# Planning a one-core decoder layer: the latest time of a load from HBM, taken from its readers or also from its queue

## The chip, the cores and the metric

The kernel runs on one core of a Trainium2 chip. The core has five engines that run side by side: TensorE (PE in the profile, with its weight loads as PEld), VectorE (DVE), ScalarE (ACT), GpSimd (POOL) and SyncE (SP). Each takes its instructions strictly in the order in which the program gives them; an instruction whose operand isn't ready holds up all that stand behind it on its engine. Two of them, SP and POOL, also issue the transfers (DMAs), which sixteen DMA engines carry out. The metric is the device time of one execution in microseconds (us).

## The reference

One decoder layer over x of shape (16, 256, 256), in float32: batch 16, length 256, width 256. Three parts follow each other, each with a residual and a layer norm after it:

- An attention by running sums: `z = x @ in_proj_w`, a causal convolution of four taps, then per head weights `p` (an exponential times a decay by position), cosines and sines of `x_val * theta`, running sums over the length of numerator and denominator, a normalisation, two small products, a gate, and `@ out_proj_w`.
- A cross attention by correlation: query, key and value are projected, correlated by Fourier transform, the five best shifts per head are chosen, and the value, shifted and weighted, goes through `Wo`.
- A mixture of eight experts of rank 64, run twice (forward and inverse): `xV * cumsum(yW)`, weighted by a router of two layers with softmax, then `U`, biases, and `@ W_O`. All its weights can be multiplied together beforehand.

## The kernel before, in words

The batch is taken in eight pairs (`NP`). For each pair the program text calls seven stages in turn: `front` (L602: xT load, input product in_ps, scores sc_ps, convolution zc, product g, broadcasts ph and gate), `body` (L668: broadcasts sn and ge, sines, scans, the products y and ss, and out_ps), `context` (L895: key and value spectra from ct, put away to HBM), `back` (L923: fetches them), `attention` (L1055), `router` (L1075) and `experts` (L1151: c_ps, v_ps, u_ps and the output). Ahead of them `fold_weights` (L815) loads twelve weight matrices as tiles `raw` and multiplies them into w_v, w_h, w_c, u_o and b_o (PE's w_ps); some twenty constants are loaded too.

None of these calls issues anything. Each engine is wrapped in `Later` (L68), and each call is noted as an `Op` with its engine, its rough duration (`cost`, L148), what it must follow and the tiles it uses. DMAs whose sources are all inputs of the program, that is loads from HBM such as xT, ct, x, raw and the constants, carry the mark `fetch` (set in `note`, L187). When all is noted, `work.run(PASSES)` plans and then issues everything in the planned order. A plan takes three passes:

- `forward` (L273) goes through time. For every engine it takes, of the operations whose inputs and tile buffers are there, the one with the smallest rank; one that is ready now goes before one that isn't. A load may not start more than 40 us (`AHEAD`, L122) before its latest time.
- `backward` (L424) goes through the plan from its end and gives each operation its latest time: what it can be moved to without making a reader late, and without making the next operation on its own engine late. SP's and POOL's queues count as engines here.
- The latest times are the ranks of the next pass. The first pass has only the ranks of `PLACES` (L39): for each stage, a length and a begin for each of the eight pairs, in units of a pair. The plan with the smallest planned end is issued.

What the order around the change depends on: the tile xT has one buffer, so the xT of a pair can be issued when the four in_ps products of the pair before are done. POOL issues the loads of constants, raw and x, and between them computes g, bothc, pp and t. SP issues xT, ct and all the broadcasts (ph, sn, ge, gate, vh, wb). The order of each queue is the plan's.

Of the kernel before, what the change touches and what calls it, by code (L numbers as in the profile page):

```python
# [36 lines left out]


PLACES = {  # L39
    "front": (1.0, 1.75, 3.7, 4.05, 4.2, 5.15, 5.65, 6.15, 8.0),  # L40
    "body": (0.5, -1.2, 1.45, 3.3, 1.4, 4.5, 4.55, 6.85, 7.75),
    "ctx": (0.9, 2.18, 0.8, 1.3, 1.6, 1.9, 1.3, 1.55, 2.55),
    "back": (0.5, -2.85, -2.95, -4.9, -5.5, -1.75, -3.0, -1.2, 2.1),
    "att": (0.1, -1.95, -2.75, -2.4, -4.5, -0.05, 0.45, 1.4, 4.15),
    "router": (1.45, 0.9, -3.2, 2.15, 2.1, 2.9, 4.65, 5.9, 4.9),
    "expert": (1.18, 4.05, 3.55, 5.65, 5.85, 7.4, 6.9, 9.8, 12.25),
    "fold": (2.75, 2.21),
}
EARLY, SLABS, XT_BUFS, ZC_BUFS, KBUFS, VBUFS, X_BUFS = 3, 17, 1, 4, 2, 3, 9
AHEAD = range(1, NP)  # L50
# [63 lines left out]
class Work:  # L114
# [309 lines left out]
    def backward(self, starts, span):  # L424

        free = dict.fromkeys(self.LEAD, span)
        late = {}
        for o in sorted(self.ops, key=lambda o: (-starts[o][1], -o.k)):
            end = min([span] + [late.get(q, span) - self.gap(o, q, q.pre[o]) for q in o.then])
            t = min(end - o.lat, free[o.eng] - o.dur + self.LEAD[o.eng])  # L430
            late[o], free[o.eng] = t, t
        return late

    def run(self, passes):
# [915 lines left out]
```

## Time and profile before

| what | value |
|---|---|
| median of 5 runs | 865.26 us (863.32 to 866.23) |
| the profiled execution | 865.74 us |
| its span in the profile | 864.0 us |
| mean granted TensorE clock | 0.979 |
| PE busy | 810.9 us, 94% of the span |
| DVE busy | 696.4 us, 81% |
| ACT busy | 596.0 us, 69% (129.6 of it loads of function tables) |
| POOL busy | 254.8 us, 29% |
| moved by DMA | 103.30 MB, mean 120 GB/s |

The profile comes from one execution. Almost all work carries the line of `give` (L452), where the planned operations are issued, so groups are told apart by tile: "in_ps<-xT,in_proj_w" is the product that writes in_ps and reads xT and in_proj_w. "A <-B x" in a list of waits says that A stood idle until x on B was done: microseconds in total, how often, and the longest. POOLq and SPq are the queues on which those engines issue DMAs. The time from a DMA's issue to its landing is part of the chain of waits where the chain runs through it.

### The profile page before, as it was taken

Reading aid. Unit: us, or ns where it says so; the run is one execution under the profiler, and the core shown is the slowest. Engines: PE = TensorE matmul, PEld = TensorE weight load, DVE = VectorE, ACT = ScalarE, POOL = GpSimd, SP = SyncE. Lnnn points to the kernel's source line nnn. Section 1 sums busy time; section 2 is a strip of 40 time slices with the busy share of each in tenths; the row PEclk is TensorE's granted clock in tenths of the full one; section 3 lists DMA queues with packets and bytes.
Section 4 is the critical chain, followed back from the end, with each engine's and each line's share of the span. In section 5 each row is a group of like instructions: output and inputs, shape, how many; then the busy total and the mean of one; then the engine's idle time right before and its main releaser. Section 6 shows DMA issues by size and latency. Waiting matters only on the chain.

```text
span 864.0 us, 12052 instructions
## 1 busy us (share of the span) xinstructions
PE 810.9 (94%) x4180; PEld 462.0 (53%) x4180; DVE 696.4 (81%) x1200; ACT 596.0 (69%) x874; POOL 254.8 (29%) x301
## 2 busy tenths in 40 slices
PE   4679999999989999999898999999999999999994
PEld 2236564464536654674353746665457357548453
DVE  6479799879899998999999799988979994472431
ACT  2859968699887999599658956769388933712601
POOL 8501455551503131424330212434122111221000
PEclk9879999999999999999999999999999999999998
DMA  7952787364745337435373536336351711130040
GB/s 233 344 121 57 184 246 202 124 186 118 191 103 129 92 86 171 111 85 147 98 171 90 131 74 142 115 77 157 84 127 45 173 46 49 38 86 1 24 98 25
DMA packets 57421, 103.30 MB, mean 120 GB/s; under 512 B 7616, under 2 KB 24032, under 8 KB 57360
## 3 DMA queue, kind: packets, MB, share of 16 engines
q1 hardware_dynamic: 47760, 71.85, 35.3%
q0 software_dynamic: 9600, 30.69, 11.0%
q8 instruction: 33, 0.54, 0.2%
q14 instruction: 28, 0.23, 0.1%
HBM read 28.06 MB, written 11.53 MB: 46 GB/s over the span
## 4 chain that ended last, share of the span: by engine, by line
PE 65%; ACT 13%; DVE 8%; issue 6%; DMA 5%; POOL 2%; POOLq 0%; SPq 0%; DVEq 0%; ACTq 0%
PE u_ps L452 11%; PE v_ps L452 10%; PE c_ps L452 9%; PE h_ps L452 6%; PE in_ps L452 4%; PE w_ps L452 3%; PE kv_ps L452 3%; PE wo_ps L452 3%; ACT L450 3%; ACT cs L452 3%; PE y L452 2%; PE ss L452 2%; PE out_ps L452 2%; DVE cs L452 2%; PE q_ps L452 2%
## 5 line engine op out<-in xcount | busy, mean ns | idle before, releaser
L450 ACT ACT_TABLE_LOAD x101 | 129.6, 1283 | 1.8
L452 PE MATMUL v_ps<-fxT,w_v 128*128 128x512 f32 x256 | 121.1, 602 | 2.8 <-DVE e L452 1.5
L452 PE MATMUL c_ps<-fcT,w_c 128*128 128x512 f32 x256 | 120.0, 601 | 0.1
L452 PE MATMUL u_ps<-u_o,e 128*128 128x256 f32 x512 | 116.4, 382 | 0.0
L452 PEld LDWEIGHTS u_ps<-u_o,e 128*128 128x128 f32 x512 | 95.6, 190 | 19.1 <-issue 6.7
L452 DVE TENSOR_TENSOR_SCAN cs<-again,cs 128x1024 f32<-128x1024 bf16 x32 | 77.3, 2416 | 0.0
L452 PEld LDWEIGHTS v_ps<-fxT,w_v 128*128 128x128 f32 x256 | 46.1, 190 | 54.6 <-issue 43.2
L452 DVE TENSOR_TENSOR_SCAN sn<-again,sn 128x1024 f32<-128x1024 bf16 x32 | 74.6, 2331 | 0.1
L452 PEld LDWEIGHTS c_ps<-fcT,w_c 128*128 128x128 f32 x256 | 46.5, 190 | 50.2 <-issue 46.8
L452 DVE SCALAR_TENSOR_TENSOR zc<-in_ps,pv,zc 128x510 f32<-128x510 f32 (+2 forms) x96 | 69.3, 734 | 2.2 <-ACT zc L452 1.7
L452 PE MATMUL h_ps<-fxT,w_h 128*128 128x512 f32 x128 | 61.5, 619 | 4.0 <-ACT fxT L452 4.0
L452 PE MATMUL kv_ps<-Wkv,specc 128*128 128x512 f32 x128 | 61.5, 614 | 3.2 <-ACT specc L452 3.2
L452 POOL TENSOR_TENSOR pp<-qf,kf 128x256 f32<-128x256 f32 (+1 forms) x32 | 43.7, 1385 | 69.5 <-ACT qf L452 64.8
L452 PE MATMUL in_ps<-xT,in_proj_w 128*128 128x512 f32 x128 | 62.9, 621 | 1.3 <-DVE sc L452 1.3
L452 DVE TENSOR_TENSOR e<-e,v_ps 128x512 f32<-128x512 f32 x64 | 43.0, 674 | 14.5 <-PE v_ps L452 14.5
L452 POOL DMA_DIRECT2D out<-x x16 | 11.7, 730 | 135.5 <-ACT x L452 123.0
L452 POOL TENSOR_TENSOR t<-vf,wf 128x256 f32<-128x256 f32 x32 | 22.7, 729 | 93.9 <-ACT wf L452 50.1
L452 ACT ACTIVATE ge<-sn 128x1024 f32<-128x1024 f32 x32 | 33.7, 1053 | 21.1 <-DVE cs L452 9.5
L452 ACT ACTIVATE sn<-sn,theta_col 128x512 f32<-128x512 f32 x64 | 44.5, 714 | 4.9 <-DMA sn<-zc 4.7
L452 DVE SCALAR_TENSOR_TENSOR cs<-cs,sn 128x1024 f32<-128x1024 f32 x32 | 42.1, 1316 | 6.9 <-ACT cs L452 6.8
L452 DVE TENSOR_TENSOR sn<-sn,ge 128x1024 f32<-128x1024 f32 x32 | 41.4, 1295 | 7.4 <-ACT sn L452 3.6
L452 ACT ACTIVATE zc<-in_ps,pv 128x512 f32<-128x512 f32 x32 | 24.5, 778 | 31.1 <-PE in_ps L452 31.1
(220 smaller groups left out, 1600.8 us busy)
## 6 DMA issues: line engine op xcount, KB each, us to landing
sn<-zc SPq DMA_DIRECT2D x64, 256.0 KB
ge<-g SPq DMA_DIRECT2D x64, 256.0 KB
wb<-fwT SPq DMA_DIRECT2D x64, 256.0 KB
ct<-in_ctx SPq DMA_DIRECT2D x16, 256.0 KB
xT<-in_xT SPq DMA_DIRECT2D x8, 512.0 KB
x<-in_x POOLq DMA_DIRECT2D x16, 256.0 KB, 3.8
ph<-sc SPq DMA_DIRECT2D x64, 64.0 KB
gate<-zc SPq DMA_DIRECT2D x64, 64.0 KB
```

The costliest lines, as they stand in the source:

```text
L450: self.scalar.preload_act_table_set(self.TABLES[table])
L452: call(*args, **kw)
```

## The change

In `backward`, an operation marked `fetch` gets its latest time from its readers alone. The latest time of the operation that stands behind it in its queue no longer bounds it, and it no longer bounds the operation that stands ahead of it. All other operations, copies out of SBUF and the fetches of spectra from HBM scratch in `back` among them, keep both bounds. Thirty-odd numbers of `PLACES`, the ranks of the first pass, are changed with it, by 0.05 to 0.25 units.

```diff
 PLACES = {
-    "front": (1.0, 1.75, 3.7, 4.05, 4.2, 5.15, 5.65, 6.15, 8.0),
-    "body": (0.5, -1.2, 1.45, 3.3, 1.4, 4.5, 4.55, 6.85, 7.75),
-    "ctx": (0.9, 2.18, 0.8, 1.3, 1.6, 1.9, 1.3, 1.55, 2.55),
-    "back": (0.5, -2.85, -2.95, -4.9, -5.5, -1.75, -3.0, -1.2, 2.1),
-    "att": (0.1, -1.95, -2.75, -2.4, -4.5, -0.05, 0.45, 1.4, 4.15),
-    "router": (1.45, 0.9, -3.2, 2.15, 2.1, 2.9, 4.65, 5.9, 4.9),
-    "expert": (1.18, 4.05, 3.55, 5.65, 5.85, 7.4, 6.9, 9.8, 12.25),
-    "fold": (2.75, 2.21),
+    "front": (1.0, 1.75, 3.7, 4.05, 4.2, 5.2, 5.65, 6.15, 8.1),
+    "body": (0.5, -1.2, 1.45, 3.3, 1.5, 4.5, 4.55, 6.85, 7.85),
+    "ctx": (0.9, 2.18, 0.8, 1.3, 1.6, 1.9, 1.3, 1.55, 2.65),
+    "back": (0.5, -2.85, -2.95, -4.9, -5.4, -1.75, -3.0, -1.2, 2.2),
+    "att": (0, -1.8, -3.0, -2.45, -4.75, -0.3, 0.2, 1.45, 4.2),
+    "router": (1.45, 0.9, -3.1, 2.15, 2.1, 2.9, 4.65, 5.9, 5.0),
+    "expert": (1.18, 3.85, 3.35, 5.45, 5.65, 7.2, 6.7, 9.6, 12.15),
+    "fold": (2.65, 2.26),
 }
...
         for o in sorted(self.ops, key=lambda o: (-starts[o][1], -o.k)):
             end = min([span] + [late.get(q, span) - self.gap(o, q, q.pre[o]) for q in o.then])
-            t = min(end - o.lat, free[o.eng] - o.dur + self.LEAD[o.eng])
-            late[o], free[o.eng] = t, t
+
+            t = end - o.lat if o.fetch else min(end - o.lat, free[o.eng] - o.dur + self.LEAD[o.eng])
+            late[o] = t
+            if not o.fetch:
+                free[o.eng] = t
         return late
```

## The prediction

> **What bounds the kernel now.** I read the page's busy times first, then TensorE's waits, then stretches of the span, then the chain and the timelines of the opening 60 us. Busy times, and the waits of TensorE (PE) and of the DVE between 20 and 60 us:
>
> ```profile
> span 864.0 us, 12052 instructions
> PE 810.9 (94%) x4180; PEld 462.0 (53%) x4180; DVE 696.4 (81%) x1200; ACT 596.0 (69%) x874; POOL 254.8 (29%) x301
> ...
> PE sc_ps L452 <- DMA xT<-in_xT: 11.6, 1, 11.6
> PE sc_ps L452 <- DMA w_sc<-in_w_sc: 8.5, 1, 8.5
> PE h_ps L452 <- ACT fxT L452: 4.0, 2, 3.1
> PE kv_ps L452 <- ACT specc L452: 3.2, 3, 2.0
> PE dft_ps L452 <- DMA f_dft<-in_f_dft: 2.6, 1, 2.6
> ...
> DVE g L452 <- DMA ph<-sc: 7.6, 1, 7.6
> ```
>
> PE is idle for 864.0 - 810.9 = 53.1 us, and its waits for DMA are all in the opening. Stretches (busy time of PE, PEld, DVE, ACT, POOL, then granted clock, DMA share, GB/s):
>
> ```profile
> 0.00:50.00 50.00, 24.42 (x96) 11.25 (x96) 26.85 (x68) 23.87 (x34) 30.94 (x52) 0.86 0.83 268
> 50.00:100.00 50.00, 50.00 (x281) 28.94 (x274) 43.44 (x44) 44.07 (x68) 9.79 (x12) 0.97 0.45 108
> ...
> 450.00:500.00 50.00, 45.91 (x259) 28.01 (x258) 44.20 (x57) 42.47 (x57) 6.76 (x7) 0.97 0.49 116
> ...
> 800.00:864.00 64.00, 52.69 (x178) 28.73 (x178) 20.86 (x50) 17.31 (x26) 3.53 (x5) 0.93 0.19 50
> ```
>
> The first 50 us hold 25.6 us of the idle time, the last 64 hold 11.3, the 750 between hold 16.2. So the kernel is bound by PE, and what can still be won lies mostly in the opening. There the chain of waits and the timelines read:
>
> ```profile
> 23.89 8.60 DMA raw<-in_V_fwd
> ...
> 36.46 12.16 DMA xT<-in_xT
> 48.66 1.93 PE sc_ps L452 x16
> ...
> 27.21 6.76 SPq L452 DMA_DIRECT2D ge<-g  x4
> 34.02 2.34 SPq L452 DMA_DIRECT2D ph<-sc  x3
> 19.47 0.73 POOL L452 DMA_DIRECT2D raw<-in_W_Q  x1
> ```
>
> PE's order is fixed, so it stood for 11.6 us until the second xT (pair 1's input) had landed. Its buffer was free when PE had finished pair 0's in_ps, at 26.5; its issue stood in SP's queue behind four ge, which wait for the DVE's g, and three ph: 10 us lost to the queue. Then it took 12.16 us among other traffic. After that idle time PE's granted clock was 0.50 from 48.6 to 52 and 0.63 to 54.
>
> **The change, part by part.** *The rule itself* (backward, L424) issues nothing; it removes from a load's due time the bound set by what stands behind it in its queue. *PLACES* only shifts the ranks of the planner's first pass. What both do is seen in the issue orders of the two programs: the same 2154 matmuls, 1192 DVE operations and 377 SP rows, but 556, 439 and 77 of them elsewhere, 290 of 772 on ACT and 66 of 301 on POOL; table loads are 101 for 102 (1.28 us each, on ACT, which is 31% idle: nothing).
>
> *POOL's queue, opening.* Ahead of raw W_Q go eleven loads fewer: ones_bd 128, Wq 256, c_corr 384, c_mean 0.5, f_roll 192, c_roll 128, x three times 256, w2t 32, out_proj_w 512: 2400 KB and 11 x about 0.6 = 6.6 us of issue time. W_Q comes at about 12.6 instead of 19.47, by adding up the 13 issues left (0.54 to 0.71 each from 1.5) and the 1.6 us bothc. *SP's queue, opening.* xT goes first and is no longer third; three of four ct (768 KB) go behind the first 30 copies. Together 3.2 MB leave the opening: at the 350 GB/s of its full slices, 9 us of transfer.
>
> *Second xT.* It now stands ahead of the four ge, behind four ph, four sn and one ph: issue when in_ps is done, 24 to 27. Landing: 6 to 12 us later, by raw loads of 256 KB (5.6 to 10.0) and its own 12.16. So 30 to 39, not 48.6. PE has work until about 31 to 35 (the same products as before, bv_ps earlier).
>
> *What is late next: the first y.* It needs the DVE chain: sn*ge, scan, cs*ge, sn*ge, scan = 1.23 + 2.28 + 1.20 + 1.22 + 2.28 = 8.2 us from the landing of ge. Before, ge went out at 27.21 and its product started at 38.30; then the DVE stood 7.6 us for ph. In the new order the operation on that ph stands behind all four scans. With ge issued at 25 to 28 and 8 to 11 us of landing, the chain starts at 34 to 38 and y comes at 42 to 46, against 55.62 before. Lead: 9.6 to 13.6 us, I take 11.5. Two matmuls of pair 1's in_ps are done ahead of it as well (1.7 us).
>
> *A new wait takes some back.* In POOL's new order the loads bt and U (five, 1.15 MB) stand behind the product g of pair 1, which waits for ACT's g and that for the DVE's zc. Before, three of the five were issued by 38.8 and the last two waited for PE alone. From y on, the DVE has 1.2 + 2 x 2.3 + 0.75 + six of 0.5 to 0.75 + 0.7 + 0.4 + 0.7 = some 11.5 us up to that zc; ACT's g is 0.8, POOL's 1.3, the issues of bt and of the first U pair 0.7 + 2 x 0.54: issued 15.5 us after y, at 57.5 to 61.5. Landing by the raw rows 5.6 to 10.0: 63 to 71.5. PE reaches their products (b_o and U_0) about 59.5 and must wait there; behind it in PE's order stand V_inv's products, whose data is there. Before, PE had done the same work by 73.4 (67.39, plus 0.9 of w_ps, 3.4 and 1.7 of in_ps). So at this point a lead of 2 to 10 us is left; I take 7.5, since the DMA is then no longer full (share 0.45 between 62 and 100) and short landings are nearer. From there PE was busy throughout up to 100 us.
>
> *Small terms.* w_sc is now fourth on POOL (1.1 us later), with less traffic beside it; PE's start, 8.5, moves by -0.5 to +1. Wo is wanted earlier by bv_ps, issued at about 5.6, landing by its row 3.2: covered by in_ps. f_dft goes out at about 9 and not at 15.5, which takes most of the 2.6. These are within the 7.5.
>
> *The loads put off* (Wq, c_corr, c_mean, f_roll, c_roll, w2t, out_proj_w, x) each stand in POOL's new order with several operations between them and their reader's data; landings are 2.8 to 5.4 us. Cost taken: nothing, covered by PE's fold and context products. If one is late, PE stands for a part of such a landing.
>
> The Trainium skill speaks against putting loads off: "DMA: Bandwidth & Descriptors", section "Rules for kernel authors", says to issue a DMA early and wait for it late. By it the early loads cost nothing, the change wins nothing, and the sum would stay at 865. The row above decides: 3.2 MB issued early shared the engines (share 1.04 between 30 and 40 us) with the one load that PE stood for.
>
> *The middle and the end.* The last 60 rows of PE's order are the same, so the 11.3 us at the end stay. In the middle every order differs, but the pace does not: PE's work ahead of each pair's out_ps, at 0.845 ns a column, is 72, 150, 227, 313, 394, 471, 572, 673 us before and 76, 150, 226, 312, 414, 481, 576, 673 now. PE stood longest (3.11 us, at 458.7) where nothing lay between the transposes fx and h_ps; that is so for one pair of eight in both orders, and elsewhere the filling is 1.7 to 3.5 us now and 0.9 to 2.8 before. So I leave the 16.2 us as they are, with -6 to +12 as bounds: about a third of it gone, or as many waits again as the largest three (3.1, 2.0, 1.8) twice over.
>
> **Sum.** The profiled execution took 865.74 us, 1.7 outside its span; 865.74 - 7.5 = 858.2. The median shown is 0.5 lower, 857.8. I say 857.5. With the outer ends (gain 2 to 13, middle -6 to +12) it could lie between 846 and 875.
>
> **Rivals.**
> 1. *The lead is eaten at bt and U*: they land near 73 us since ge, zc or the landing are late. Price: 0 to 4 us won, 861 to 866. For it: POOL waits in order, and landings of 8.4 us (median of raw) were common. Against: the DMA has 3 MB less to carry. From about 73.4 on, nothing is left.
> 2. *The middle turns to waiting for the DVE* (slower). The DVE is 94 to 97% busy in stretches such as 250:300 (48.69 of 50); if its 439 moved operations put 2.3 us scans ahead of what PE waits for (v_ps waited for e three times, y for cs once, up to 0.9 each), ten such waits more outweigh 7.5 us, and twelve to twenty give 868 to 875. Against: pace and filling are as before, and the DVE gets its inputs 9 us earlier too.
> 3. *The middle absorbs the lead*: PE reaches 150 us sooner, but the DVE's work ahead of each pair does not. That gives 864 to 866. It is told from 1 by the lead at 75 us.
>
> **Chances.** Forecast (gain of 4 to 13): 0.60, 852 to 861. More, with a calmer middle: 0.08, below 852. Rivals 1 and 3 together: 0.15, two fifths of it still more than 0.2% faster. Rival 2: 0.17. A measurement here tells 0.2%, or 1.7 us. Faster 0.74, same 0.09, slower 0.17. Range 849 to 868: the forecast, rivals 1 and 3, and the near edges of the others.
>
> **What would show it.** PE's wait for xT falls from 11.6 to under 5; the first y comes at 42 to 46; the DVE's 7.6 us for ph is gone; a new PE wait of some 3 to 8 us for raw bt or U stands near 60 to 70 us; PE's idle time in 0:100 falls from 25.6 to about 18, and in 100:800 stays near 16. I am wrong if PE has as much idle time up to 100 us as before, or if the middle's moves by more than 8.

## The result and the profile after

The changed kernel takes 867.69 us (median of 34 runs, 862.55 to 872.55), the kernel before 864.86 us on the same chips (60 runs). The ratio is 1.004, with a 95% interval of 1.003 to 1.0049: slightly slower. The forecast was 857.5 us and faster. The profiled execution took 870.86 us, 3.2 more than the median, with a span of 868.9.

The page of the changed kernel, its head:

```profile
span 868.9 us, 12046 instructions
...
PE 818.0 (94%) x4180; PEld 464.2 (53%) x4180; DVE 692.6 (80%) x1200; ACT 594.8 (68%) x873; POOL 262.4 (30%) x301
```

TensorE (PE) is idle for 868.9 - 818.0 = 50.9 us, 2.2 less than before, and yet the span is 4.9 longer: the same 4180 matmuls were busy for 7.1 us more. The list of PE's waits (total, times, longest, in us):

```profile
PE sc_ps L455 <- DMA w_sc<-in_w_sc: 7.5, 1, 7.5
PE y L455 <- DVE cs L455: 5.1, 5, 1.5
PE in_ps L455 <- DMA xT<-in_xT: 4.2, 1, 4.2
PE kv_ps L455 <- DVE dx L455: 2.1, 1, 2.1
PE w_t_ps L455 <- DVE ks L455: 2.1, 1, 2.1
...
PE dft_ps L455 <- POOL bothc L455: 1.7, 2, 1.3
...
PE w_ps L455 <- DMA raw<-in_bt: 0.7, 1, 0.7
```

The wait for the second xT fell from 11.6 to 4.2 us, f_dft's 2.6 is gone, and the new wait for bt is 0.7. Waits for the DVE, hardly present before, now stand near the top. PE's timeline of the opening (start, duration, what, idle time before it):

```profile
34.37 3.75 PE L455 MATMUL in_ps<-xT,in_proj_w 128*128 128x512 f32 x4 [4.21 <-DMA xT<-in_xT]
...
46.28 0.64 PE L455 MATMUL y<-sn,w_ri 128*32 128x256 f32 x8
...
63.25 1.10 PE L455 MATMUL w_ps<-raw 128*128 128x256 f32 x4 [0.66 <-DMA raw<-in_bt]
```

The first y came at 46.28 us (55.62 before). So the opening did nearly what was predicted. Stretches of the span, columns as in the prediction:

```profile
0.00:50.00 50.00, 33.94 (x149) 16.03 (x150) 34.70 (x72) 29.75 (x44) 20.74 (x37) 0.93 0.68 201
50.00:100.00 50.00, 45.84 (x236) 25.78 (x235) 40.01 (x45) 45.91 (x70) 20.79 (x25) 1.00 0.67 175
...
150.00:200.00 50.00, 44.30 (x252) 26.27 (x251) 44.84 (x73) 41.91 (x68) 28.21 (x33) 0.90 0.53 145
...
800.00:868.90 68.90, 57.62 (x205) 32.93 (x203) 20.86 (x50) 17.89 (x27) 3.53 (x5) 0.95 0.18 46
```

Up to 100 us PE is idle for 20.2 us (25.6 before), after 800 us for 11.3 (11.3 before), and between them for 19.4 (16.2 before).

Stretches of fixed times do not say where a lead is lost, because after a lead each stretch holds other work. So both traces were lined up by work: each matmul of the trace was given the usual spacing of its kind (429 ns for 128x512, 216 for 128x256 and so on, from the same traces; 741 us in all), and the table has the time at which PE had so much of it behind it. All columns but the first are differences to before, in us; the experiments' columns are used below. A column is one execution: that of after lies 3.2 us above its kernel's median, that of before (865.74) 0.9 above, that of "loads and g" (854.98) 2.9 below.

```
work    before  after  rule   table  loads  loads  after  after  nudge  nudge
                       alone  alone  moved  and g  late   out    a      b
 40      75.8   -8.6   -8.8   -5.6   -0.2   -8.3   -3.3   -8.5   -0.7   -2.5
100     142.1   -5.0   -7.0   -0.1   +1.7   -7.0   -3.4   -9.4   +3.1   -0.8
140     189.3   +2.2   -3.5   -0.2   -0.3   -9.2   +3.9   -2.8   +0.4   -1.4
200     260.7   -1.3   -4.1   -3.3   -1.9  -10.8   +0.6   -6.2   +1.3   -5.0
300     369.6   +0.3   -0.2   -3.2   -1.8  -10.6   +2.2   -4.4   +2.1   -4.7
400     489.0   -2.6   -3.0   -6.0   -0.2  -10.6   -2.1  -10.0   +3.4   +4.4
500     595.9   +1.5   +2.2   +8.6   -0.3  -10.8   +3.6   -3.9  +14.0   +3.3
600     706.1   +4.4   +5.1  +10.3   -0.3  -10.8   +7.7   +0.4  +21.0  +10.8
700     811.0   +4.9   +5.6  +10.4   -0.3  -10.8   +8.2   +1.0  +28.8  +24.3
```

Column "after": the lead at 75 us is real, 8.6 us, and the end is 4.9 us late. From work 40 to work 600 before takes 630.1 us and after 643.2 to 643.5 for the same products. In these executions the middle gave back 13 us; by the medians (2.8 us slower at the end in spite of the lead of 8.6) it is 11. Of the 13, by the same alignment, 5.2 are more idle time of PE (16.1 to 21.3), 4.6 are more time at a lower granted clock (5.1 to 9.7), and some 3 are not accounted for. The idle time also changed its cause: waits that the DVE ended went from 2.9 us (7 waits) to 14.3 (18 waits), those that ACT ended from 11.3 to 4.5.

### The profile page after: what moved, and what is told of

It is laid out like the page before. It is cut to its first block, busy times and chain, and to the rows that moved or that the text cites. A ratio compares the mean times of both kernels' runs of the same rounds, so it can differ in the third digit from the quotient of the medians.

```text
span 868.9 us, 12046 instructions
## 1 busy us (share of the span) xinstructions
PE 818.0 (94%) x4180; PEld 464.2 (53%) x4180; DVE 692.6 (80%) x1200; ACT 594.8 (68%) x873; POOL 262.4 (30%) x301
## 5 line engine op out<-in xcount | busy, mean ns | idle before, releaser
L455 DVE TENSOR_TENSOR_SCAN cs<-again,cs 128x1024 f32<-128x1024 bf16 x32 | 75.4, 2357 | 0.0
L455 PEld LDWEIGHTS c_ps<-fcT,w_c 128*128 128x128 f32 x256 | 46.4, 190 | 54.1 <-issue 46.9
L455 POOL TENSOR_TENSOR t<-vf,wf 128x256 f32<-128x256 f32 x32 | 29.1, 928 | 118.7 <-ACT wf L455 76.0
L455 PE MATMUL h_ps<-fxT,w_h 128*128 128x512 f32 x128 | 59.6, 602 | 2.1 <-ACT fxT L455 1.3
L455 POOL TENSOR_TENSOR pp<-qf,kf 128x256 f32<-128x256 f32 (+1 forms) x32 | 39.5, 1251 | 55.8 <-ACT qf L455 55.8
L455 POOL TENSOR_TENSOR x<-dx 128x256 f32<-128x256 f32 x32 | 33.1, 1053 | 51.6 <-DVE dx L455 39.0
L455 DVE TENSOR_TENSOR cs<-cs,ge 128x1024 f32<-128x1024 f32 x32 | 43.8, 1370 | 2.5 <-ACT cs L455 2.4
```

Of the source, the lines that this page charges most:

```text
L455: call(*args, **kw)
```

## The experiments

The question is why the middle gave back 11 to 13 us. Three answers were put up. A: the lead is worth its size, and the new order of the middle costs these 11 to 13 us by itself. B: the middle absorbs any lead, because something else sets its pace. C: the loads that the rule puts off come too late. Each run stands against before on the same chip.

**Only the loads of the opening are moved.** Before's plan is kept, and behind the planner a few lines move loads in the finished order; TensorE, the DVE and ACT have before's orders to the last instruction. One run moves loads on both queues, one on SP's alone.

```diff
-        self.give(best[1], best[2])
+        self.give(self.moved(best[1]), best[2])
...
+        at = order.index(raw[-1]) + 1
+        order[at:at] = late
...
+        order.insert(order.index(sp[0]), xts[0])
...
+        order.insert(min(order.index(o) for o in ge), xts[1])
```

> The plan of before, with the orders of TensorE, DVE and ACT untouched to the last instruction; only the loads of the opening stand where the new rule puts them: on POOL's queue Wq, c_corr, c_mean, f_roll, c_roll, w2t, out_proj_w and three x go behind the last raw U load and ones_bd behind the fourth raw W_fwd, on SP's queue xT goes first, the second xT ahead of the four ge and two ct behind ph. So raw bt and U keep their old places. Theory A (the lead of the opening is real, some 8 us at 75 us, and it is the new order of the middle that gives it back): the old middle keeps most of it, 855 to 860 us. Theory B (the middle is set by the DVE's work and absorbs any lead of TensorE, whatever the order): 862 to 866, with the lead gone by 350 us. Theory C (loads put off land too late and hold back the middle): 865 or more, with waits of POOL or TensorE for ct, Wq, c_corr, f_roll or x that before does not have.

> As the run with both queues changed, but POOL's queue is as before: the eleven loads (2400 KB) still go out early, and only SP's queue has the second xT ahead of the four ge. Theory A: the second xT is issued at about 26 instead of 36.5 but shares the engines with the 2400 KB; TensorE's wait for it falls from 11.6 to some 4 to 8 us, and 858 to 863 us. Were the SP queue the whole of the opening's gain, this run and the one with both would agree within 1.7 us. Theory B: 862 to 866.

Both queues: 866.7 us, ratio 1.0019 (1.0004 to 1.0033). SP alone: 865.06 us, 1.0005 (0.999 to 1.002). A, which expected 855 to 860 for both queues, seemed to fall. But the column "loads moved" shows that the lead never reached the middle: it was 11.7 us at 42 us and gone at work 40. The DVE's timeline of the run with both queues says why:

```profile
39.24 1.23 DVE L489 TENSOR_TENSOR sn<-sn,ge 128x1024 f32<-128x1024 f32 x1 [4.68 <-DMA ge<-g]
47.11 0.75 DVE L489 SCALAR_TENSOR_TENSOR g<-g,dw,ph 128x512 f32<-128x512 f32 x1 [6.65 <-DMA gate<-zc]
47.78 2.28 DVE L489 TENSOR_TENSOR_SCAN sn<-again,sn 128x1024 f32<-128x1024 bf16 x1
```

and PE's timeline what became of it:

```profile
50.12 1.08 PE L489 MATMUL y<-sn,w_ri 128*32 128x256 f32 x8 [5.40 <-DVE sn L489]
54.57 1.08 PE L489 MATMUL y<-cs,w_ri 128*32 128x256 f32 x8 [3.37 <-DVE cs L489]
```

The scan had its input at 40.5 and stood behind g until 47.8. (The profile names the copies of gate here as what g waited for; in before's row it was ph, which comes over the same queue. g started at 47.1 in both.) In before, PE's wait for xT ended at 48.7 and the DVE's wait for ph at 47.1: two waits of 11.6 and 7.6 us beside each other, each of which hides the other. The runs so far tested the opening, not the middle.

**The DVE's g goes behind the scans as well.** On top of both queues one DVE operation is moved, behind the second scan in one run, behind the fourth (where after has it) in the other.

```diff
+        g = dve[scans[0] - 1]
...
+        order.remove(g)
+        at = order.index(dve[scans[behind]]) + 1
...
+        order.insert(at, g)
```

> As the run with both queues changed, whose lead of 11.7 us at 42 us was gone at the first y, because the DVE's g (which stood for ph until 47.1 us) is placed ahead of the scans; here that one DVE operation goes behind the second scan, and TensorE's, ACT's, POOL's and SP's orders are as in that run. The scans then start at about 40.5 and not 47.8, and the first y comes at about 43 to 44, the second at 48 (50.1 and 54.6 there). All theories: a lead of 5 to 8 us over before at 75 us. Theory A (before's order of the middle keeps TensorE busy, so a lead goes through it): 857 to 861 us. Theory B (whatever the order, the middle waits for the DVE's chain and absorbs the lead): the lead shrinks to 0 to 2 us by 212 us, as in after and in the run with the rule alone, and the time is 863 to 866.

> As the run with the DVE's g behind the second scan, but g goes behind the fourth, which is where after has it. The second pair of scans is some 0.7 us earlier, and g, with all that follows from it for pair 1 (ACT's g, the next ge), some 6 us later. Theory A: 857 to 862. Theory B: 863 to 866. If g's place matters by itself, this run is 1 to 3 us slower than the other.

Behind the second scan: 858.82 us, ratio 0.9921 (0.9896 to 0.9946). Behind the fourth: 857.93 us, 0.9903 (0.9879 to 0.9927). This is the fastest kernel of the study, 7.7 us below before's 865.61 on that chip. g's place among the scans makes no difference that these intervals can tell. DVE and PE of the second one:

```profile
39.94 2.29 DVE L501 TENSOR_TENSOR_SCAN sn<-again,sn 128x1024 f32<-128x1024 bf16 x1
...
52.10 0.72 DVE L501 SCALAR_TENSOR_TENSOR g<-g,dw,ph 128x512 f32<-128x512 f32 x1
```

```profile
43.54 0.64 PE L501 MATMUL y<-sn,w_ri 128*32 128x256 f32 x8
46.74 0.64 PE L501 MATMUL y<-cs,w_ri 128*32 128x256 f32 x8 [2.56 <-DVE cs L501]
```

g no longer waits for anything, and y comes at 43.5. The lead at work 40 is 8.3 us, the same as after's 8.6, and here the middle does not absorb it: column "loads and g" has 10.8 us of it from work 200 to the end, the medians 7.7. B has fallen, and C with it for the loads of the opening, since nearly the same ones are put off here. The rule puts off later loads as well, which this run leaves where they were; but by the lists of waits the only load from HBM that an engine waits for between 75 and 706 us is ct, for 9.1 us in after, 9.8 in this run and 5.8 in before, nearly all of it on POOL. PE's waits between 75 and 700 us in this run are nearly before's (h_ps for fxT, 3.9, against 4.0; w_f_ps for wT, 2.0 in both):

```profile
PE h_ps L501 <- ACT fxT L501: 3.9, 2, 3.0
PE kv_ps L501 <- ACT specc L501: 2.7, 3, 1.5
PE w_f_ps L501 <- ACT wT L501: 2.0, 1, 2.0
```

**The lead taken from after.** After's plan, with the four ge and three ph issued ahead of the second xT again.

```diff
+        move = ge + ph
+        order = [o for o in order if o not in move]
+        at = order.index(xt)
+        order[at:at] = move
```

> After's plan with one thing undone: on SP's queue the second xT is issued behind the four ge and three ph again, as in before; all other queues are as in after. TensorE's wait for this xT goes from 4.2 to some 10 to 14 us, and the lead of 8.4 us at 75 us falls to 0 to 4. Theory A (the lead is worth its size at the end, and after's own middle has lost 13 us beside it): 5 to 8 us slower than after, 873 to 877. Theory B (the middle absorbs a lead): within 2 us of after, 866 to 870.

873.03 us, ratio 1.0077 (1.0051 to 1.0103). PE's waits:

```profile
PE in_ps L473 <- DMA xT<-in_xT: 12.8, 1, 12.8
```

The wait grew by 8.6 us, the lead at work 40 shrank by 5.3, and 3.3 of that is left at work 700. The ratio is 0.0037 above after's 1.004, which is 3.2 us, and 0.8 to 5.6 by the two intervals: less than A's 5 to 8, more than B's 2. So in after's order, too, more than half of a lead seems to pass to the end.

**The two halves of the change, and nudges of the table.** The new rule with the old table, the old rule with the new table (28 of its numbers differ), and twice the old rule with one number of the old table changed by 0.05.

```diff
-    "expert": (1.18, 4.05, 3.55, 5.65, 5.85, 7.4, 6.9, 9.8, 12.25),
+    "expert": (1.18, 4.0, 3.55, 5.65, 5.85, 7.4, 6.9, 9.8, 12.25),
```

```diff
-    "expert": (1.18, 4.05, 3.55, 5.65, 5.85, 7.4, 6.9, 9.8, 12.25),
+    "expert": (1.18, 4.05, 3.55, 5.6, 5.85, 7.4, 6.9, 9.8, 12.25),
```

> The new backward rule with the old table of ranks. The planner then makes a third order: an opening like that of after, 382 of 2154 matmuls placed elsewhere than in before. Theory A: TensorE's wait for xT is under 5 us and the lead at 75 us is some 6 to 10 us; what is left of it is a matter of this order's own middle, 855 to 868. Theory B: 862 to 866. Theory C: 867 or more, like after, since the same loads are put off by the same rule.

> The old backward rule with the new table of ranks: loads go out early as in before, 616 of 2154 matmuls are placed elsewhere. All theories: no lead of the opening, TensorE waits 9 to 12 us for the second xT. Theory A (the order of the middle decides the rest, and after's middle is bad because it was planned anew): 862 to 875, not below before by more than 0.2%. Theory C (the loads put off are the cost): 864 to 867, since the loads are not put off here.

> Before with one rank of the table changed by 0.05 (the experts of one pair, 4.05 to 4.0): no rule changed, no load meant to move; the planner makes a plan with 939 rows of TensorE's order different. Theory A, in the form that any new plan of the middle costs (before's is 735 us from work 40 to the end of the middle, the three others 749 to 752): 870 to 880, since there is no lead of the opening. If the loss is the rule's or the new table's own, 864 to 867.

> As the other nudge, with another rank (5.65 to 5.6, the experts of another pair): 981 rows of TensorE's order differ. If any new plan costs: 870 to 880. If the loss is the rule's or the table's own: 864 to 867.

Rule alone: 868.37 us, 1.0037 (1.0015 to 1.0059). Table alone: 878.48 us, 1.0163 (1.0143 to 1.0183). Nudge a: 894.38 us, 1.0337 (1.0313 to 1.0361). Nudge b: 890.18 us, 1.0285 (1.0261 to 1.0309). The rule alone lies just above A's 855 to 868 and would fit C; but the table alone, which puts no load off, lost more, where C expected 864 to 867. (It also has a lead of 5.6 us at work 40, which no theory expected; its wait for the second xT is 8.2 us.) The table and the nudges came out dearer than expected: some 25 to 30 us for a step of 0.05 that moves no load by intent. PE's waits in the run of nudge a:

```profile
PE sc_ps L452 <- DMA xT<-in_xT: 11.7, 2, 8.3
PE wt_ps L452 <- POOL lg L452: 9.7, 4, 7.5
```

The opening's stall for xT is still there, and wt_ps waits 9.7 us for POOL's lg in place of before's 1.8. In all five plans that the planner made anew (after's among them) PE takes 643 to 652 us from work 40 to work 600, where before's order takes 630; the two nudges lose another 8 and 13.5 us after work 600, where the others lose nothing. So such a loss needs neither the rule nor its loads: it came with every new plan. Before's order is the good one of the six; why it is so much better than its neighbours, no run here shows.

**One join of after's middle.** Between work 60 and 140, where after goes from 7.8 us ahead to 2.2 behind, pair 0's out_ps stood on PE behind two dft_ps groups. Their bothc came late since on POOL they stood behind the issue of a read-back of vf, which went out at 97.6 us, when the write of vf had landed; their ct had landed by 92.8, so it was not ct, as the expectation below has it. In the run out_ps goes ahead of both groups, and the copies of their results go along; nothing else moves.

```diff
+        order = [o for o in order if o not in dft + read]
+        at = order.index(out[-1]) + 1
+        order[at:at] = dft + read
```

> After's plan with one step of TensorE moved: pair 0's out_ps goes ahead of the two dft_ps groups whose bothc waits for POOL and ct. In after out_ps stood behind them until 100.8 us and ran at half clock (5.2 us for 3.7), and the DVE stood 6.9 us for it. Now out_ps starts at about 98.5 and the DVE's x at about 102.5 instead of 106.1. If this join is where after's middle begins to lose (a third of the 13 us): 2 to 4 us faster than after, 863 to 866. If the loss is spread over many joins, each with its own release: 0 to 1.5 us faster than after, 866 to 868.

866.08 us, ratio 1.0007 (0.9987 to 1.0028); the ratio is 0.003, or 3 us, below after's. Stretches of after around that place:

```profile
97.00:100.50 3.50, 1.83 (x15) 1.45 (x13) 1.62 (x2) 3.47 (x6) 2.88 (x5) 1.00 0.48 125
100.50:104.00 3.50, 3.50 (x19) 2.70 (x19) 0.00 (x0) 1.96 (x5) 1.69 (x3) 0.51 0.66 191
```

and of the run:

```profile
97.00:100.50 3.50, 3.28 (x30) 2.47 (x27) 1.42 (x3) 2.98 (x6) 3.48 (x6) 1.00 0.59 157
100.50:104.00 3.50, 3.50 (x21) 2.54 (x21) 3.41 (x11) 1.70 (x3) 0.80 (x2) 1.00 0.75 221
```

PE had stood for 1.67 us in two waits for bothc, its next 3.5 us ran at a granted clock of 0.51, and the DVE did nothing in them, because it waited 6.9 us for out_ps. With out_ps ahead that wait is 2.1 us (DVE's waits, after and then the run):

```profile
DVE x L455 <- PE out_ps L455: 6.9, 1, 6.9
```

```profile
DVE x L471 <- PE out_ps L471: 2.1, 1, 2.1
```

Column "after out" is 4.4 us better than "after" at work 100 and 3.9 at work 700. So one join holds a quarter to a third of the 13 us. The rest lies in others that were not taken apart (between work 400 and 600, for one, after loses another 7).

**What each part of the opening is worth.** The fastest run with POOL's queue as in before, and before with the DVE's g moved alone.

> The run with g behind the fourth scan (857.9 us), but POOL's queue is before's: the eleven loads of 2400 KB go out early again, so this tests by itself what the rule does on POOL's queue. Left are the second xT ahead of the four ge on SP, two ct behind ph, and the DVE's g behind the scans. If the 2400 KB beside ge and xT cost what the prediction said (up to 9 us of transfer), ge lands later and the time is 861 to 865. If only the order on SP and on the DVE counts, it is within 2 us of the run with both queues: 857 to 860.

> Before with one DVE operation moved and nothing else: g, which stands 7.6 us for ph ahead of the scans, goes behind the fourth scan; all loads stay where before has them, so the second xT is still issued behind the four ge. In before TensorE stands for xT until 48.7 us and the DVE for ph until 47.1 us. If the two waits lie beside each other, each hides the other: the scans are done early, but TensorE still gets xT at about 48.7 and its first y at about 55, so 863 to 866, no change. If the DVE's wait were a cost of its own, it would give 4 to 7 us: 858 to 861.

SP's queue and g: 859.04 us, 0.9935 (0.9913 to 0.9957). g alone: 863.49 us, 0.9995 (0.9976 to 1.0014). PE's timeline with g alone:

```profile
49.07 1.94 PE L467 MATMUL sc_ps<-xT,w_sc 128*32 128x256 f32 x16 [6.63 <-DMA xT<-in_xT]
...
56.17 0.64 PE L467 MATMUL y<-sn,w_ri 128*32 128x256 f32 x8
```

So g alone gives nothing, SP's loads alone give nothing (1.0005), and both together give 0.65%: neither wait shows its price while the other stands. Putting off POOL's eleven loads of 2400 KB adds 2.8 us by the two ratios, and anything from 0 to some 6 by their intervals; the first y came at 46.9 us with these loads early and at 43.5 with them put off, and the lead at work 40 is 6.1 and 8.3 us.

## Why the prediction was wrong

**The sum.** It had two terms: a lead of 7.5 us and a middle left as it was, "with -6 to +12 as bounds". The size of the lead is right: 8.6 us in after, and a kernel that has such a lead with the old middle takes 857.93 us where 857.5 was forecast. In part that is luck. After's lead came by other terms, 9.3 us at the first y instead of 11.5, and hardly any of the 4 us that bt and U were to take back; and the kernel of 857.93 us leaves bt and U in their old places. The step that failed is the second, "every order differs, but the pace does not", and "So I leave the 16.2 us as they are". It measured +11 us by the medians and +13 in the profiled executions, at or beyond the far one of its bounds.

**Why that step was wrong.** It judged the middle by PE's work ahead of each pair's out_ps and by the filling at h_ps. Neither says when the DVE, ACT and POOL deliver, and that is where the new waits lie. The bound counted idle time alone; 4.6 of the 13 us were products run at a lower clock. And it took a middle that stays as it is for the likeliest outcome of an unseen new order, with 0.17 for one that is slower. Five new plans were measured, and all five were worse in the middle, by 13 to 22 us from work 40 to work 600.

**Point by point.**
- raw W_Q, said for 12.6 us, was issued at 11.5. PE began at 7.5, half a us before the earliest time named (8.5 - 0.5).
- The second xT, said for 24 to 27 and a landing of 30 to 39, was issued at 25.3, and PE had it at 34.4. Its wait was 4.2 us, under the 5 named.
- The first y, said for 42 to 46, came at 46.3 (25 to 28 and 8 to 11 add up to 33 to 39 for the chain's start, not 34 to 38, and so to 41 to 47); the DVE's 7.6 us for ph are gone.
- The new wait at bt and U, said for 3 to 8 us, was 0.7. They were issued at 58.6 to 61.5, at the late edge of 57.5 to 61.5, but 128 KB of bt landed in 4.5 us, under the 5.6 to 10.0 that was taken from the raw rows of the crowded opening, and PE came to it at 62.6 and not at 59.5. PE waited 3.2 us for ACT's w_v and w_h instead, which had no term.
- PE idle up to 100 us: 20.2, said about 18. In 100:800: 19.4, said near 16. By the prediction's own test ("if the middle's moves by more than 8") this would have passed, since the test read idle time in fixed stretches. Only the alignment by work shows the 13 us.
- The loads put off in the opening cost nothing that shows, as said: a kernel that puts nearly the same ones off is the fastest.
- The price of the early loads was mis-sized: 9 us of transfer was the argument for the change against the Trainium skill's rule ("DMA: Bandwidth & Descriptors", section "Rules for kernel authors": issue early, wait late). With the 2400 KB early, xT still reached PE within 9.6 us of its issue (27.4 to 37.0 in the run with SP's queue alone), and within 9.5 without them (25.9 to 35.4). As putting them off is worth some 2.8 us and not 9, the rule was nearer than the row. What cost most was the place in SP's queue, behind ge, and that is a limit of issuing early that a queue in order sets.
- Rival 3, that the middle absorbs any lead, is refuted for before's order; in after's order at most a part is absorbed. Rival 1 did not come.

Rival 2 is what came, "ten such waits more": waits ended by the DVE went from 7 to 18. Over the whole stretch the DVE did not become fuller: it is busy for less of 100:700 in after than in before, as the windows of before and of after say (third number):

```profile
100.00:700.00 600.00, 583.86 (x3165) 329.62 (x3164) 551.78 (x913) 474.82 (x682) 193.75 (x210) 0.99 0.52 129
```

```profile
100.00:700.00 600.00, 581.28 (x3104) 328.02 (x3108) 538.35 (x903) 465.26 (x670) 192.62 (x207) 0.98 0.52 128
```

But just ahead of these waits it is full, as the rival had it. Of the 18 waits 14 are over 0.1 us, 14.0 us together. For ten of them, 9.6 us, the DVE was busy for at least 4.9 of the 5 us before the operation that PE stood for was done, and eight of these ten had, wholly or in part, a scan in that stretch that PE was not waiting for. Before's waits were of the same kind (five of six over 0.1 us), but fewer. An example, DVE and then PE of after:

```profile
424.59 1.21 DVE L455 TENSOR_TENSOR cs<-cs,ge 128x1024 f32<-128x1024 f32 x1
425.73 0.67 DVE L455 TENSOR_TENSOR gate<-gate,y 128x512 f32<-128x512 f32 x1
426.32 2.28 DVE L455 TENSOR_TENSOR_SCAN sn<-again,sn 128x1024 f32<-128x1024 bf16 x1
428.53 2.26 DVE L455 TENSOR_TENSOR_SCAN cs<-again,cs 128x1024 f32<-128x1024 bf16 x1
...
430.84 0.64 PE L455 MATMUL y<-cs,w_ri 128*32 128x256 f32 x8 [1.54 <-DVE cs L455]
```

So at these places PE waits for what stands ahead in the DVE's order. That the DVE's own earlier waits, such as the 6.9 us for out_ps up to 106 us, put it behind there is possible, and not shown.

What stays open: some 3 of the 13 us, which are neither idle time nor the clock, the joins after work 140, and what makes before's order the better one.

## What to carry to other kernels

Where a planner orders the work, a change of its rule is two changes: the local one that is meant, and a new draw of everything else. Here the local one was worth some 8 us, and the five draws cost some 11 to 30, so price the draw by nudging a number that should do nothing, and test the meant part with the old order held fixed. Two waits that end at about the same time can hide each other: here removing either gave nothing, and only both together showed the price.

## What the runs showed of the hardware

A pause of PE can cost twice, and which pauses do follows a grid. Up to the last products, the granted clock fell to half for whole multiples of 3.41 us (3.41, 6.83, 13.65), and within a trace all these stretches lie on one grid of 3.41 us. In the fourteen profiles, leaving out the first 10 us, 86 windows of that grid had 2.0 us or more of PE's idle time, and each of them was followed by a window at half clock. From full clock, no window with less than 1.4 us was followed by one. Of 66 in between, 24 were. In after the window 97.1 to 100.5 us had 1.67 us of idle time, and the next ran at 0.51: out_ps took 5.2 us instead of 3.7.

So by these counts two short waits in one window can cost 1.7 us more, and the same two in different windows nothing. Over work 40 to 600 after lost 9.7 us to the clock beside 21.3 us of idle time, before 5.1 beside 16.1, the fastest kernel 1.7 beside 16.5. The traces of the seven kernels that have before's order of the middle lost 1.7 to 5.1 us to the clock there, so part of the fastest kernel's 10.8 us in the table is luck of where its pauses fall.

The Trainium skill ("TensorE: Matmul & The Clock Gate", section "Part 1: The HAM clock gate (the "warmup" mystery)") has the same free-running window, but says that the clock drops after an idle window. Here a window that was little more than half idle was enough.
